# Attention in a graph network kernel: seven products of quarters for values, queries and keys, and 1/z by way of memory

## The chip, the cores and the metric

The kernel runs on one core of one Trainium2 chip. The metric is the time of one execution on the device in microseconds (us); less is better. A profile is one further execution, in which the hardware records when each instruction began and ended. In the profile's words PE is TensorE (PEld its weight loads), DVE is VectorE, ACT is ScalarE, POOL is GpSimd and SP is SyncE, which here only issues DMAs.

## The reference

Everything is float32. `x` has 1250 rows (nodes, later tokens) of 768 numbers. Two graph attention layers come first, then a transformer block with attention and a mixture of eight experts. Cut to what is touched here:

```python
x = x + gat_layers(layernorm(x), edges)            # 41250 edges
y = layernorm(x)
y = y + attention(layernorm(y, g1, b1))
y = y + moe(layernorm(y, g2, b2))                  # 8 experts, the top 2 of each token
out = x + y

def attention(a):                                  # T = 1250, H = 12 heads of HD = 64
    q, k, v = split((a @ Wqkv).reshape(T, 3, H, HD))
    scores = einsum('qhd,khd->hqk', q, k) * HD ** -0.5
    return einsum('hqk,khd->qhd', softmax(scores), v).reshape(T, D) @ Wproj
```

## The kernel before

**Sizes.** D = 768 columns are DC = 6 pieces of P = 128; the 1250 rows are NT = 10 tiles of T = 125. DH = 384. The matrix engine contracts over the partitions, so the normed rows are kept turned over: `yT` is 128 x 6 x 1250, the transposed input of the attention; the graph stage makes it tile by tile (L597 to L600). `v`, the values, is 125 x 10 x 768, rows on partitions. `wv` (the values' weights) and `wp` (Wproj) share one slot of the pool `wpool`, so `wp` is loaded after the last use of `wv`. `aT` is the attention's output, transposed like `yT`.

**Values (L653 to L660).** `value_rows(t)` makes one tile of 125 rows: two halves of 384 columns, six accumulated products each, evicted from PSUM by ACT.

**Queries and keys (L626 to L645).** `queries_keys(p)` serves a pair of heads p (0 to 5). It loads 128 columns of the keys' weights and 128 of the queries' (`wqk`), then goes through the 1250 rows in three chunks of 417, 417 and 416 columns (`CHUNKS`). For each chunk it makes keys and then queries with six accumulated products each. The keys use the PSUM bank with the tag "mb", the queries the one with the tag "pz", and ACT evicts each with a multiply, which puts the factor 1/8 (HD to the power -0.5) on the queries. It is a Python generator that yields after each product, so the caller (`go`, L647) hands out one product at a time among other work.

**A unit (L665 to L738)** is a pair of heads p and a chunk k of 417 queries; there are 18, in the order p, k. Its methods:
- `scores(j)`: for tile j of 125 keys, one product per head into a double bank `st`; ACT copies it to `sT` in a ring of 15 slots; DVE keeps the running maximum `most` (L687), which reads `st` itself.
- `top()`: eight transposes of `most` on PE and a reduction on DVE give one maximum per query; `row()`: eight more products spread it over the partitions into the bank `mb`.
- `weights(j)`: DVE subtracts `mb` (L708), ACT takes the exponential (L709), POOL adds up the ten tiles into `acc` (L714).
- `values(j)`: products of the weights with `v` into the bank `pav`. `sums` multiplies `acc` by ones, which gives z, the sum of a query's weights, on every partition of the head (bank `pz`). `divide()`: DVE takes 1/z of 128 x 417 (L737) and multiplies (L738).

**Order.** PE's instructions in the attention are in the order of the program text (`manual_schedule`, L744 and L764). The instructions of the other engines are put in order by a scheduler, except where `keep_in_program_order` pins one. First come two tiles of values, then all of the first pair's queries and keys, then the ten scores of unit 0, each followed by a tile of values (L745 to L753). Then the loop over units (L756): the head of a unit is two products of the next pair's queries and keys, `top` of the unit, `divide` of the one before, four more products, the first score of the next unit, and `row`. After the head it goes by two tiles at a time: the next unit's two scores, two products of queries and keys in the first three rounds, the weights two tiles ahead, the values. So the 36 products of a pair are spread over the three units before it is used, twelve in each. The last pair's three units have none to do.

**Queues.** SP issues the loads of `wqk` and, later, half of the reload of the rows `xs` from memory (L915); ACT issues the other half between its own instructions. POOL's queue carries the zero fill of `xd` (L618 to L624): eight large DMAs from one tile of zeros, and a small one; they prepare the experts' slots, which are filled and read after the attention. After the attention the projection takes `aT` by tiles (`product`, L925), adds it to the rows and goes on to routing and experts.

Of the kernel before, what the change touches and what calls it, by code (L numbers as in the profile page):

```python
# [27 lines left out]
def gnn_ffn_kernel(  # L28
# [69 lines left out]
    xsd = dram.tile([N, D], F32, name="xsd")  # L98
    xd = dram.tile([NE * REG + P, RW], F32, name="xd")
# [503 lines left out]
    attn = late.enter_context(tc.tile_pool(name="attn", bufs=1))  # L603
    aT = attn.tile([P, DC, N], F32, name="aT")
    with tc.tile_pool(name="att", bufs=2) as ap, \
            tc.tile_pool(name="aps", bufs=2, space=PSUM) as aps, \
            tc.tile_pool(name="apm", bufs=1, space=PSUM) as apm, \
            tc.tile_pool(name="apa", bufs=1, space=PSUM) as apa:
# [7 lines left out]


        zero = ap.tile([P, RW], F32, name="zero", bufs=1)  # L618
        nc.gpsimd.memset(zero, 0.0)  # L619
        nc.gpsimd.memset(zero[:, D:D + 1], float(NOWHERE))  # L620
        for e in range(NE):
            nc.gpsimd.dma_start(xd[e * REG:(e + 1) * REG, :].rearrange("(p r) d -> p r d", p=P),
                                zero[:, None, :].to_broadcast([P, REG // P, RW]))
        nc.gpsimd.dma_start(xd[NOWHERE:NOWHERE + P, :], zero)  # L624

        def queries_keys(p):  # L626

            wqk = ap.tile([P, DC, 2, P], F32, tag="wqk", name="wqk", bufs=1)
            for i in (1, 0):
                nc.sync.dma_start(wqk[:, :, i, :], Wqkv[:, i * D + p * P:i * D + (p + 1) * P].rearrange(  # L630
                    "(c p) f -> p c f", p=P))
            qk = ap.tile([P, 2, N], F32, tag="qk", name="qk")
            yield qk
            for c0, w in CHUNKS:
                for i in (1, 0):
                    if i == 1:
                        pq = apm.tile([P, 2, 512], F32, tag="mb", name="pk")[:, 0, :]
                    else:
                        pq = apa.tile([P, 512], F32, tag="pz", name="pq")
                    for c in range(DC):  # L640
                        nc.tensor.matmul(pq[:, :w], wqk[:, c, i, :], yT[:, c, c0:c0 + w],  # L641
                                         start=(c == 0), stop=(c == DC - 1))
                        if c == DC - 1:
                            nc.scalar.mul(qk[:, i, c0:c0 + w], pq[:, :w], 1.0 if i == 1 else HD ** -0.5)
                        yield None  # L645
# [98 lines left out]
        with tc.manual_schedule(engines={mybir.EngineType.PE}):  # L744
            for t in range(BEFORE):  # L745
                value_rows(t)
            for _ in steps:
                pass
# [417 lines left out]
```

## Time and profile before

| | us |
|---|---|
| median of three runs (lowest to highest) | 1517.28 (1515.45 to 1519.91) |
| profiled execution, its own time | 1518.66 |
| profiled execution, span of the core | 1516.8 |
| busy in the span: PE | 1437.4 (95%) |
| busy in the span: PE weight loads, beside it | 784.6 |
| busy in the span: DVE | 808.4 (53%) |
| busy in the span: ACT | 574.4 (38%) |
| busy in the span: POOL | 418.4 (28%) |
| mean clock granted to PE, of full | 0.965 |

The span divides into the graph layers (to 554), the front of the attention with values, first queries and keys and first scores (554 to 673), the units (673 to 1180.7), and projection, routing and experts (to the end). By these stages:

| us from the start | PE busy | DVE busy | ACT busy | POOL busy | PE clock | GB/s |
|---|---|---|---|---|---|---|
| 554 to 673 | 116.80 | 15.83 | 22.44 | 9.05 | 1.00 | 293 |
| 673 to 1080 | 401.53 | 315.57 | 241.04 | 247.39 | 1.00 | 12 |
| 1080 to 1180.7 | 90.61 | 80.64 | 60.74 | 63.88 | 0.95 | 39 |

The parts of a profile are read as follows. The rows by engine divide the span into 40 slices and give the busy share of each in tenths; the row PEclk gives the clock of PE in tenths of full. A group's line has the line of the code, engine and operation, what it writes and reads with the shapes (partitions x elements), how often, the busy time in all and the mean in ns, and the idle time of the engine just ahead of these instructions. A line of the timeline has the start, the duration, the engine and the operation; x8 says that eight like instructions are drawn together, and a bracket names what a wait ended with. A line of windows has the stretch, its length, and the busy time and count of PE, PEld, DVE, ACT and POOL; after them the clock of PE, the share of the DMA engines that were busy and GB/s.

### The profile page before, as it was taken

The numbers are of one execution on the slowest core, as the hardware profiler recorded it, in microseconds if no ns is written. First come the engines' busy times: TensorE is split into PE (matmuls) and PEld (weight loads), VectorE is DVE, ScalarE is ACT, GpSimd is POOL, SyncE is SP. The second block draws the span as 40 slices with busy tenths as digits, with TensorE's granted clock in tenths as the row PEclk, the third lists the DMA queues.
The fourth block names the chain that finished last, engine by engine and source line by source line (L and its number), as shares of the span: only waits on it lengthen the run. The fifth ranks groups of instructions, "written<-read, shape, count | busy, mean of one in ns | idle before, by whom it ended". The sixth has DMA issues, their size and how long they took to land. (4 is left out here: it accounts for less than half of the span.)

```text
span 1516.8 us, 15936 instructions
## 1 busy us (share of the span) xinstructions
PE 1437.4 (95%) x5990; PEld 784.6 (52%) x5990; DVE 808.4 (53%) x1287; ACT 574.4 (38%) x915; POOL 418.4 (28%) x278
## 2 busy tenths in 40 slices
PE   6787999999999999999999999999988999899997
PEld 4574555556555555553343344344333666665654
DVE  6688456434036650127778778777878654111111
ACT  4220613205116521226646656655656223221211
POOL 5000000000000010006656655665666222222222
PEclk9758999999999999999999999999999998899999
DMA  7000020000021129940000000000030323565653
GB/s 208 22 2 11 11 73 0 0 28 5 3 100 42 60 81 383 373 152 0 22 1 0 22 1 21 1 22 0 4 99 1 134 107 136 215 234 171 229 187 124
DMA packets 48198, 124.58 MB, mean 82 GB/s; under 512 B 5629, under 2 KB 22207, under 8 KB 48120
## 3 DMA queue, kind: packets, MB, share of 16 engines
q1 hardware_dynamic: 31468, 57.35, 11.6%
q0 software_dynamic: 11968, 56.21, 10.2%
q10 hardware_dynamic: 4684, 9.99, 2.2%
q8 instruction: 48, 0.79, 0.2%
q14 instruction: 30, 0.25, 0.0%
HBM read 70.46 MB, written 57.55 MB: 84 GB/s over the span
## 5 line engine op out<-in xcount | busy, mean ns | idle before, releaser
L714 POOL TENSOR_TENSOR acc<-acc,sT 125x834 f32<-125x834 f32 (+1 forms) x139 | 272.9, 1963 | 10.9
L526 PE MATMUL pagg<-h,wt 125*125 125x385 f32 (+1 forms) x800 | 263.5, 486 | 0.4 <-DVE wt L519 0.4
L687 DVE TENSOR_TENSOR most<-most,st 125x834 f32<-125x834 f32 (+1 forms) x144 | 146.9, 1020 | 107.1 <-ACT sT L681 104.2
L526 PEld LDWEIGHTS pagg<-h,wt 125*125 125x125 f32 x800 | 147.0, 187 | 104.7 <-DVE wt L519 3.5
L708 DVE TENSOR_TENSOR sT<-sT,mb 125x834 f32<-125x834 f32 (+1 forms) x180 | 174.1, 1014 | 22.6 <-PE mb L703 22.6
L709 ACT ACTIVATE sT<-sT 125x834 f32<-125x834 f32 (+1 forms) x180 | 158.4, 900 | 49.3 <-DVE sT L708 48.9
L681 ACT COPY sT<-st 125x834 f32<-125x834 f32 (+1 forms) x180 | 151.6, 848 | 53.9 <-PE st L678 52.1
L678 PE MATMUL st<-qk 64*125 64x417 f32 (+1 forms) x720 | 164.8, 558 | 4.0 <-DVE most L687 4.0
L722 PE MATMUL pav<-sT,v 125*64 125x417 f32 (+1 forms) x720 | 151.8, 534 | 9.4 <-ACT sT L709 9.4
L619 POOL MEMSET zero<- 128x771 f32 x1 | 0.7, 740 | 529.7 <-PE ptr L143 529.7
L714 POOL TENSOR_TENSOR acc<-sT 125x834 f32<-125x834 f32 (+1 forms) x18 | 35.4, 1964 | 275.9 <-ACT sT L709 275.9
L678 PEld LDWEIGHTS st<-qk 64*125 64x125 f32 x720 | 56.8, 185 | 99.4 <-issue 43.2
L722 PEld LDWEIGHTS pav<-sT,v 125*64 125x64 f32 x720 | 42.8, 137 | 106.3 <-issue 44.4
L900 PE MATMUL poe<-we,hT 128*128 128x384 f32 x264 | 89.8, 486 | 0.0
L641 PE MATMUL pq<-yT,wqk 128*128 128x417 f32 (+1 forms) x216 | 88.1, 534 | 0.0
L867 PE MATMUL phe<-xT,we 128*128 128x384 f32 (+1 forms) x288 | 86.6, 460 | 0.0
L929 PE MATMUL po<-wp,aT 128*125 128x384 f32 x240 | 86.5, 497 | 0.0
L641 PE MATMUL pk<-yT,wqk 128*128 128x417 f32 (+1 forms) x216 | 84.0, 526 | 0.0
L206 PE MATMUL ph<-gw,xnT 128*125 128x384 f32 x240 | 81.6, 500 | 0.8 <-DMA gw<-in_L_gnn_W_dram 0.8
L657 PE MATMUL pv<-wv,yT 128*125 128x384 f32 x240 | 79.9, 490 | 1.4 <-issue 1.4
L206 PE MATMUL ph<-gw,x1T 128*125 128x384 f32 x240 | 79.2, 491 | 0.0
L530 DVE RECIPROCAL rz<-pagg 125x1 f32<-125x1 f32 x20 | 3.3, 166 | 141.4 <-PE pagg L526 141.4
(225 smaller groups left out, 1718.5 us busy)
## 6 DMA issues: line engine op xcount, KB each, us to landing
xd<-zero POOLq DMA_DIRECT2D x8, 3855.0 KB, 15.7
we<-in_L_ffn_W_dram SPq DMA_DIRECT2D x16, 1152.0 KB
xr<-xd SPq DMA_DIRECT2D x25, 385.5 KB
gw<-in_L_gnn_W_dram SPq DMA_DIRECT2D x2, 2304.0 KB
wqk<-in_L_ffn_Wqkv_dram SPq DMA_DIRECT2D x12, 384.0 KB
xres<-in_x_dram SPq DMA_DIRECT2D x10, 375.0 KB
xsd<-xres ACTq DMA_DIRECT2D x10, 375.0 KB
xn<-in_x_dram SPq DMA_DIRECT2D x9, 336.0 KB
```

The source lines that it names most:

```text
L206: nc.tensor.matmul(po[:, s, :DH], xT[:, c, t * T:(t + 1) * T], w[:, c, s * DH:(s + 1) * DH], start=(c == 0), stop=(c == DC - 1))
L526: nc.tensor.matmul(po[:, s, :DH + s], ws[j][:, (d - d0) * T:(d - d0 + 1) * T], h[:, j, s * DH:(s + 1) * DH + s], start=(j == 0), stop=(j = ...
L641: nc.tensor.matmul(pq[:, :w], wqk[:, c, i, :], yT[:, c, c0:c0 + w], start=(c == 0), stop=(c == DC - 1))
L678: nc.tensor.matmul(st[:T, i, :w], self.qk[r, 1, j * T:(j + 1) * T], self.qk[r, 0, self.c0:self.c0 + w], start=True, stop=True)
L681: nc.scalar.copy(s[:, :, :w], st[:T, :, :w])
L687: nc.vector.tensor_tensor(self.most[:, :, :w], prev[:, :, :w], st[:T, :, :w], ALU.max)
L708: nc.vector.tensor_tensor(s[:, :, :w], s[:, :, :w], self.mb[:T, :, :w], ALU.subtract)
L709: nc.scalar.activation(s[:, :, :w], s[:, :, :w], AF.Exp)
L714: nc.gpsimd.tensor_tensor(self.acc[:, :, :w], prev[:, :, :w], s[:, :, :w], ALU.add)
L722: nc.tensor.matmul(self.pav[r, :w], v[:, j, hd0:hd0 + HD], s[:, i, :w], start=(j == 0), stop=(j == NT - 1))
L867: nc.tensor.matmul(ph[:, :n * P], w1[:, c, f * P:(f + 1) * P], xT[:, c, :], start=(c == 0), stop=(c == DC - 1))
L900: nc.tensor.matmul(po[:, d, :DH], hT[:, f, s * P:(s + 1) * P], w2[:, f, d * DH:(d + 1) * DH], start=(f == 0), stop=(f == FC - 1))
```

## The change

**Seven products in place of eight.** A product of two matrices cut into quarters needs eight products of quarters. The new code makes seven, of sums and differences of quarters, and puts the result together by additions (`seven`). The contraction of 768 is cut into two halves of KH = 3 pieces, the 1250 rows into two halves of NH = 625, and the weights' columns into two halves: 384 each for the values, and queries and keys (128 each) for a pair of heads. One of the seven products is three accumulated matrix instructions. Values: five rounds (a tile of the first half of the rows with the matching one of the second) of 21 products of 384 columns, which stand in place of 24. Queries and keys: two pieces of 313 and 312 columns, each with 21 products. A round has one ACT copy (product 1, kept in `u1`) and seven DVE additions, each of which reads PSUM and an earlier part and writes a part or the result.

**The sums** are POOL's. `left_sums` makes three new matrices and changes one quarter of the weights in place; they lie in the memory of `aT`, under the name `spare`. `right_sums` does the same with `yT` and makes `t2`, `t3` and `t4`. The left sums of the values and all right sums come first on POOL, then two memsets, the first pair's left sums, and the zero fill's DMAs. `t2` and `t3` are in a pool that closes after the values; two POOL copies put them into `kept`, in the slot of `wv` and `wp`. The pool `sx` then takes their memory for five of the fifteen score slots, which are now tags of their own. `wp` is loaded before unit 15.

**Order.** `go(steps, 1)` hands out one product of seven (three matrix instructions): two in the head of a unit and one in each of the first three rounds. A pair has 14 products for 15 such places. FREE and BOUND give the order of the seven and the PSUM bank of each: m and n are the two halves of "mb", z is "pz" and v is "pav". In the front all values' first round precedes the first pair's queries and keys, and the other four rounds follow the ten scores, as even as may be.

**1/z.** `divide` now has ACT copy z and the unscaled output out of PSUM (to `zs` and `aT`). SP writes one row of z per head to memory (`zd`), and reads them back as 120 partitions of 7 (`self.z`). One unit later, in the round j = 4, `invert` takes the reciprocal on DVE, writes it to memory (`zr`) and reads it back twice, once for each head's 64 partitions (into `kept`, or into `yT` for the last three units). `scale`, after the next unit's `top`, multiplies on POOL. The last unit keeps the reciprocal and the multiply of before. The factor 1/8 is now in the exponential.

The pools `att` and `attn` now take over memory tile by tile (`reuse_waits="tile"`), and `most` and `acc` have one buffer where they had two. The functions and blocks taken out are printed above; what is put in, and the lines of the units:

```diff
...
+    ZW = 420
+    zd = dram.tile([3 * H // 2, 2, ZW], F32, name="zd")
+    zr = dram.tile([3 * H // 2, 2, ZW], F32, name="zr")
...
+        spare = aT.rearrange("p c n -> p (c n)")
+        KH = DC // 2
+        NH = N // 2
+        def parts(flat, w, n):
+            return [flat[:, i * KH * w:(i + 1) * KH * w].rearrange("p (c k) -> p c k", c=KH) for i in range(n)]
+        def left_sums(a, w, flat, pin=False):
+            place = tc.keep_in_program_order if pin else lambda ins: ins
+            s1, s2, s4 = parts(flat, w, 3)
+            a11, a12, a21, a22 = (a[:, c:c + KH, f:f + w] for f in (0, w) for c in (0, KH))
+            place(nc.gpsimd.tensor_tensor(s1, a21, a22, ALU.add))
+            place(nc.gpsimd.tensor_tensor(s2, s1, a11, ALU.subtract))
+            place(nc.gpsimd.tensor_tensor(s4, a12, s2, ALU.subtract))
+            place(nc.gpsimd.tensor_tensor(a21, a11, a21, ALU.subtract))
+            return [a11, a12, s4, a22, s1, s2, a21]
+        y11, y12, y21, y22 = (yT[:, c:c + KH, n0:n0 + NH] for c in (0, KH) for n0 in (0, NH))
+        t4 = ap.tile([P, KH, NH], F32, name="t4", bufs=1)
+        def right(t2, t3):
+            return [y11, y21, y22, t4, y12, t2, t3]
+        def right_sums(t, t2, t3):
+            q = slice(t * T, (t + 1) * T)
+            nc.gpsimd.tensor_tensor(t3[:, :, q], y22[:, :, q], y12[:, :, q], ALU.subtract)
+            nc.gpsimd.tensor_tensor(y12[:, :, q], y12[:, :, q], y11[:, :, q], ALU.subtract)
+            nc.gpsimd.tensor_tensor(t2[:, :, q], y22[:, :, q], y12[:, :, q], ALU.subtract)
+            nc.gpsimd.tensor_tensor(t4[:, :, q], y21[:, :, q], t2[:, :, q], ALU.subtract)
+        FREE = ["1m", "6n", "2z", "7v", "5m", "4n", "3z"]
+        BOUND = ["1m", "2n", "6z", "7z", "4z", "5m", "3n", "1z", "2z", "6z", "7m", "4n", "5z", "3z"]
+        def seven(order, operands, np_, w, o11, o12, o21, o22):
+            def part(i):
+                return ap.tile([P, DH], F32, tag=f"u{i}", name=f"u{i}", bufs=1)[:np_, :w]
+            u4 = None
+            p1, u2, u3 = (part(i) for i in (1, 2, 3))
+            for i, name in order:
+                if name == "m":
+                    two = apm.tile([P, 2, 512], F32, tag="mb", name="mq")
+                if name in "mn":
+                    b = two[:np_, "mn".index(name), :w]
+                else:
+                    b = apa.tile([P, 512], F32, tag={"z": "pz", "v": "pav"}[name], name="q")[:np_, :w]
+                for c in range(KH):
+                    lhs, rhs = operands(int(i) - 1, c)
+                    nc.tensor.matmul(b, lhs, rhs, start=(c == 0), stop=(c == KH - 1))
+                if i == "5":
+                    u4 = part(1)
+                if i == "1":
+                    nc.scalar.copy(p1, b)
+                for o, u in {"2": [(o11, p1)], "6": [(u2, p1)], "7": [(u3, u2)], "4": [(o21, u3)],
+                             "5": [(u4, u2), (o22, u3)], "3": [(o12, u4)]}.get(i, []):
+                    nc.vector.tensor_tensor(o, b, u, ALU.add)
+                yield None
+        QW = -(-NH // 2)
+        PIECES = [(0, QW), (QW, NH - QW)]
+        def queries_keys(p, ys, free):
+            wqk = ap.tile([P, DC, 2 * P], F32, tag="wqk", name="wqk", bufs=1)
+            for i in (0, 1):
+                nc.sync.dma_start(wqk[:, :, i * P:(i + 1) * P], Wqkv[:, (1 - i) * D + p * P:(1 - i) * D + (p + 1) * P].rearrange(
...
+            ws = left_sums(wqk, P, spare[:, (4 + p % 2) * N:], pin=True)
...
+            for i, (c0, w) in enumerate(PIECES):
+                h0, h1 = slice(c0, c0 + w), slice(NH + c0, NH + c0 + w)
+                yield from seven(FREE if free else BOUND[7 * i:7 * i + 7],
+                                 lambda k, c: (ws[k][:, c, :], ys[k][:, c, h0]), P, w,
+                                 qk[:, 1, h0], qk[:, 1, h1], qk[:, 0, h0], qk[:, 0, h1])
         def go(steps, n):
...
+        def value_rows(t, ws, ys):
+            return seven(FREE, lambda k, c: (ys[k][:, c, t * T:(t + 1) * T], ws[k][:, c, :]), T, DH,
+                         v[:, t, :DH], v[:, t + NU, :DH], v[:, t, DH:], v[:, t + NU, DH:])
...
+        zs = ap.tile([P, ZW], F32, name="zs", bufs=1)
+        nc.vector.memset(zs, 1.0)
+        ZQ = 7
+        ZP = 2 * ZW // ZQ
+        def inverses(n):
+            at = n % 2 * ZW
+            if n < len(units) - NCK:
+                return kept[:, 2 * KH * NH + at:2 * KH * NH + at + ZW]
+            return yT.rearrange("p c n -> p (c n)")[:, at:at + ZW]
+        RING = 15
+        rings = [ap] * NT + [None] * (RING - NT)
...
+                self.first = (p * NCK + k) * NT
...
-                s = ap.tile([T, 2, CW], F32, tag="sT", name="sT", bufs=15)
+                r = (self.first + j) % RING
+                s = rings[r].tile([T, 2, CW], F32, tag=f"sT{r}", name="sT", bufs=1)
...
-                    self.most = ap.tile([T, 2, CW], F32, tag="most", name="most")
+                    self.most = ap.tile([T, 2, CW], F32, tag="most", name="most", bufs=1)
...
             def weights(self, j):
...
-                nc.scalar.activation(s[:, :, :w], s[:, :, :w], AF.Exp)
+                nc.scalar.activation(s[:, :, :w], s[:, :, :w], AF.Exp, scale=HD ** -0.5)
...
-                    self.acc = ap.tile([T, 2, CW], F32, tag="acc", name="acc")
+                    self.acc = ap.tile([T, 2, CW], F32, tag="acc", name="acc", bufs=1)
...
-            def divide(self):
+            def divide(self, n):
...
+                self.o = aT[:, self.p, self.c0:self.c0 + w]
+                if n + 1 == len(units):
+                    nc.vector.reciprocal(zs[:, :w], self.pz[:, :w])
+                    nc.vector.tensor_tensor(self.o, self.pav[:, :w], zs[:, :w], ALU.mult)
+                    return
+                nc.scalar.copy(zs[:, :w], self.pz[:, :w])
+                nc.scalar.copy(self.o, self.pav[:, :w])
+                for i in range(2):
+                    nc.sync.dma_start(zd[n, i:i + 1, :], zs[i * HD:i * HD + 1, :])
+                self.z = small.tile([ZP, ZQ], F32, tag="z", name="z", bufs=1)
+                nc.sync.dma_start(self.z, zd[n].rearrange("i (a b) -> (i a) b", b=ZQ))
+            def invert(self, n):
+                tc.keep_in_program_order(nc.vector.reciprocal(self.z, self.z))
+                nc.sync.dma_start(zr[n].rearrange("i (a b) -> (i a) b", b=ZQ), self.z)
+                self.rz = inverses(n)
+                for i in range(2):
+                    nc.sync.dma_start(self.rz[i * HD:(i + 1) * HD, :], zr[n, i:i + 1, :].to_broadcast([HD, ZW]))
+            def scale(self):
+                tc.keep_in_program_order(nc.gpsimd.tensor_tensor(self.o, self.o, self.rz[:, :self.w], ALU.mult))
+        with tc.tile_pool(name="tsum", bufs=1, reuse_waits="tile") as tp:
+            t2, t3 = (tp.tile([P, KH, NH], F32, name=f"t{i}") for i in (2, 3))
+            ws = left_sums(wv, DH, spare)
+            for t in range(NU):
+                right_sums(t, t2, t3)
+            zero = spare[:, 3 * N:3 * N + RW]
+            tc.keep_in_program_order(nc.gpsimd.memset(zero, 0.0))
+            tc.keep_in_program_order(nc.gpsimd.memset(zero[:, D:D + 1], float(NOWHERE)))
+            steps = queries_keys(0, right(t2, t3), True)
+            qks = [next(steps)]
+            for e in range(NE):
+                tc.keep_in_program_order(nc.gpsimd.dma_start(
+                    xd[e * REG:(e + 1) * REG, :].rearrange("(p r) d -> p r d", p=P),
+                    zero[:, None, :].to_broadcast([P, REG // P, RW])))
+            tc.keep_in_program_order(nc.gpsimd.dma_start(xd[NOWHERE:NOWHERE + P, :], zero))
+            with tc.manual_schedule(engines={mybir.EngineType.PE}):
+                for _ in value_rows(0, ws, right(t2, t3)):
+                    pass
+                for _ in steps:
+                    pass
+                rest = [r for t in range(1, NU) for r in [value_rows(t, ws, right(t2, t3))] * len(FREE)]
+                u = Unit(0, 0, qks[0])
+                for j in range(NT):
+                    u.scores(j)
+                    for r in rest[len(rest) * j // NT:len(rest) * (j + 1) // NT]:
+                        next(r)
+            kept = wpool.tile([P, DC, D], F32, tag="w", name="kept").rearrange("p c d -> p (c d)")
+            ys = right(*parts(kept, NH, 2))
+            nc.gpsimd.tensor_copy(ys[5], t2)
+            nc.gpsimd.tensor_copy(ys[6], t3)
+        sx = ring.enter_context(tc.tile_pool(name="sx", bufs=1, reuse_waits="tile"))
+        rings[NT:] = [sx] * (RING - NT)
...
+        waiting = []
...
-                    steps = queries_keys(p + 1)
+                    steps = queries_keys(p + 1, ys, False)
...
+                else:
+                    wp = load_big_weight(Wproj, "wp")
...
             with tc.manual_schedule(engines={mybir.EngineType.PE}):
-                go(steps, 2)
+                go(steps, 1)
...
-                    last.divide()
-                go(steps, DC - 2)
+                    last.divide(n - 1)
+                for old in waiting:
+                    old.scale()
+                go(steps, 1)
                 if nxt is not None:
...
                     if j < 6:
-                        go(steps, 2)
+                        go(steps, 1)
...
+                    if j == 4 and last is not None:
+                        last.invert(n - 1)
+                        waiting = [last]
...
-        last.divide()
+        last.divide(n)
+        for old in waiting:
+            old.scale()
...
```

## The prediction

> **What bounds the kernel now.** I began with the page's rows by time: TensorE (PE) is over 90% busy from slice 7 to slice 28, which holds the whole attention, and its clock there is full.
>
> ```profile
> PE   6787999999999999999999999999988999899997
> PEclk9758999999999999999999999999999998899999
> ```
>
> Next the groups, for who else is near the bound, and what each removed instruction takes.
>
> ```profile
> L714 POOL TENSOR_TENSOR acc<-acc,sT 125x834 f32<-125x834 f32 (+1 forms) x139 | 272.9, 1963 | 10.9
> L708 DVE TENSOR_TENSOR sT<-sT,mb 125x834 f32<-125x834 f32 (+1 forms) x180 | 174.1, 1014 | 22.6 <-PE mb L703 22.6
> L641 PE MATMUL pq<-yT,wqk 128*128 128x417 f32 (+1 forms) x216 | 88.1, 534 | 0.0
> L737 DVE RECIPROCAL rz<-pz 128x417 f32<-128x417 f32 (+1 forms) x17 | 46.8, 2755 | 0.0
> L738 DVE TENSOR_TENSOR aT<-pav,rz 128x417 f32<-128x417 f32 (+1 forms) x17 | 10.0, 590 | 0.5
> ```
>
> Every fp32 product is two instructions (216 where the code has 108), and a mean of 534 ns is a latency: consecutive ones start 350 ns apart (weight loads at 573.18, 573.53, ...), 0.84 ns a column. Third, the order in time of one unit of attention. Fifteen of the eighteen units with query/key work start 28.9 us apart; here is the second half of one.
>
> ```profile
> 776.20 1.67 PE L678 MATMUL st<-qk 64*125 64x417 f32 x8
> 776.39 2.89 DVE L708 TENSOR_TENSOR sT<-sT,mb 125x834 f32<-125x834 f32 x3
> 777.80 1.67 PE L641 MATMUL pq<-yT,wqk 128*128 128x417 f32 x4
> 779.19 1.02 DVE L687 TENSOR_TENSOR most<-most,st 125x834 f32<-125x834 f32 x1
> 780.66 1.02 DVE L687 TENSOR_TENSOR most<-most,st 125x834 f32<-125x834 f32 x1 [0.45 <-ACT sT L681]
> 780.95 1.76 PE L678 MATMUL st<-qk 64*125 64x417 f32 x8
> 791.24 2.76 DVE L737 RECIPROCAL rz<-pz 128x417 f32<-128x417 f32 x1
> ```
>
> PE has no gap, but VectorE (DVE) has none either from the first subtraction (767.05) to 780.2: a pair of scores needs its bank freed by the maximum two before it, and the one that frees the second bank at 781.68 is on time by 0.1 us. The 2.76 us reciprocal is in the unit's head, where DVE waits anyway. Last, the clock: the last three units have no query/key work, and PE idles in them.
>
> ```profile
> 1110.00:1113.00 3.00, 1.26 (x8) 0.49 (x6) 3.00 (x4) 1.92 (x3) 0.00 (x0) 1.00 0.99 255
> 1113.00:1116.00 3.00, 2.27 (x8) 0.49 (x8) 3.00 (x4) 1.51 (x3) 1.22 (x1) 0.67 0.19 60
> 1116.00:1120.00 4.00, 4.00 (x12) 1.46 (x12) 3.34 (x4) 3.27 (x5) 3.84 (x3) 0.50 0.00 0
> ```
>
> After 3 us with PE 1.26 us busy the clock (third column from the right) is halved for some 7 us.
>
> **Part 1, the front (554.5 to the first maxima transposes at 672.97).** Values: 240 instructions of 384 columns become 210. They start 0.330 us apart (24 from 643.13 to 651.06): 69.3 us. First pair's queries and keys: 72 x 0.350 = 25.2 becomes 84 of 312.5 columns x 0.84 ns = 0.262: 22.0. The ten score pairs stay at 0.97 each, 9.7, and one first step of the next pair is 6 x 0.262 = 1.6. But today PE starts values at 555.8, ahead of the last transposes (562.1); in the changed order the first product follows them, and waits until ScalarE (ACT) has evicted the last of yT, at 564.9. So 564.9 + 69.3 + 22.0 + 9.7 + 1.6 = 667.5, against 672.97: -5.5. PE will have idled from 554.5 to 564.9 but for 0.83 us. Here a rule bears: the Trainium skill, "TensorE: Matmul & The Clock Gate" (Part 1, the HAM clock gate), says that one idle window of about 3.4 us halves the clock and one busy window restores it. The rule would charge 1.7 us (half speed for one window), the row 3.5 (for 7 us); I take 2.5: **-3.0**.
>
> The sums go on GpSimd (POOL), idle there. A sum of two operands takes 1.96 us for 834 elements, 2.35 ns each. The values' left sums (4 x 1152 elements, 10.8 us) can start once the last weights are made on DVE (521.8), ending at 532.6; of 20 right sums (0.88 each), the last four wait for the last eviction and end at 568.4; memsets and the first left sums of the pair (0.84 + 4 x 0.90) at 572.9. The pair's products begin at about 581: 8 us of cover; gone, each us late is a us on PE. The zero-fill (8 large DMAs and a small one, 31 MB) moves past all these on POOL's queue, from 564.3 to 572.9, and ends at about 671 instead of 662; its rows are read after 1200. Into it falls the second pair's weight load (786 KB, 4 us of transfer at 750.6 when alone), wanted at 668 and issued at about 603: nothing.
>
> **Part 2, the first unit.** Two POOL copies of 1875 elements (t2, t3 to `kept`) start when the last fourth product ends, 3.6 us before the first maxima transposes; five score slots lie in the memory that they leave. No copy by POOL is in the trace. The memset (0.74 us for 771) gives 1.8 us each, the two-operand sum 4.4. "GPSIMD Engine Reference" (4.1, engine selection) puts one-input work near line rate, so I take 1.8. They end at +0.0 (+5.2 by the sum), and the first ACT copy to such a slot is at +4.3: 0 to 1; **+0.5**.
>
> **Part 3, fifteen units.** A pair of heads has three units (k = 0, 1, 2), and fourteen products of 1.57 us replace 36 matmuls: 25.2 - 22.0 = 3.2 us less PE. It is not spread evenly.
> - Head (maxima transposes to row): eight instructions and their waits took 2.99 us (790.87 to 793.86); one product takes 1.6: -1.39. The step ahead of the transposes grows from 1.40 to 1.57: +0.16.
> - Loop: three slots of 1.40 become products of 1.57, in k = 2 only two.
> - DVE loses the reciprocal and the multiply (3.35, in the head, hidden) and gets fourteen additions of PSUM and SBUF per pair. None is in the trace. The nearest row is the 417-column multiply, 0.59; with 1.02 for 834 that is 0.16 fixed + 1.03 ns a column, so 0.48 for 313, and 0.42 in a queue where 834-wide ones start 0.94 apart instead of 1.02. Bounds: nothing, where DVE has idle time, and 0.84.
> - Walking one unit with these: k = 0 and 1: PE's slots give +0.5 of which 0.3 vanishes in waits that are there now (pav waits for the exponential): -1.39 + 0.16 + 0.22 = -1.0. k = 2: three additions and the small reciprocal (0.15) come before the maximum that frees the second bank: it ends at 782.6 instead of 781.68, while PE, with no third product, arrives 1.5 us sooner: it waits 1.35 and then 1.2 us. Its first score also waits for the addition that completes the query rows, +0.65. Sum -0.24.
> - A pair: -2.24; five pairs: **-11.2** (PE alone: -16).
> - The clock in k = 2: PE is busy 0.7 of 3.25 us. By the skill's rule there is no idle window (the gap is broken by a score pair), so nothing is lost; by the row (1.26 of 3 sufficed) half speed follows, up to 3 us. The row decides on this chip; some waits hide it: 1 us each, **+5** (0 to 15).
> - The eviction now waits: ACT copies pz and pav (0.52 each) in place of its two qk evictions: even. 1/z goes through memory: two writes, a read, a DVE reciprocal of 120x7, a write, two broadcasts, 6 DMAs on SP per unit. With 3.05 us a hop (the row of `out_dram<-soon`), z lands at 2.5 + 6.2 = 8.7 us after the transposes and is inverted after the eighth subtraction, at 16.6; behind it wait two subtractions and all later maxima, and PE behind them. Cover 7.9 us. In k = 2 the read stands behind the weight load (4 us): still covered. The scaling on POOL comes a unit later, 5 us after its broadcast landed.
> - POOL: left sums 3.6 per pair and scaling 1.0 per unit before the first `acc`, which waits for ACT 10.6 us today; even.
> - The scale 1/8 moves into the exponential: nothing.
>
> **Part 4, the units without such work.** In the last three the reciprocal is not hidden: PE's row ends at 1110.36 and the subtraction starts at 1111.39, the multiply sits between the first two. Without: 1.0 + 0.4 in each of two units, and about half of the 2.2 and 0.8 us lost to the halved clock: **-4**. The third is filled with Wproj matmuls: nothing. Wproj's load moves from before the second pair to after unit 14's scaling: unit 15's small DMAs queue behind 2.4 MB (some 7 us), z lands at about 14: still before 16.6.
>
> **Part 5, the tail.** The last two 1/z lie in yT's memory, so the reload of xs (20 DMAs on SP and ACT, today from 1097.6) waits for the last scaling, 19 us into the last unit. The first rows land at +22, wanted at +25 (1184.3), and behind the waiting issues ACT has only the square root of 1189; **+0.5** (0 to 2). `first_w` then shares the rings; it is wanted 60 us later.
>
> **Sum**: -3.0 + 0.5 - 11.2 + 5 - 4 + 0.5 = -12.2. The profiled execution's span goes from 1516.8 to 1504.6, its own time from 1518.66 to 1506.5; the median shown is 1.4 lower, 1517.28, so 1505.
>
> **Rivals.**
> A, DVE's additions fit into its waits: the whole PE saving arrives, no clock loss: -5.5 - 16 - 5 = -26.5, 1491. For it: DVE is 22.7 of 28.3 us busy in a unit. Against: its idle time lies in the last two iterations.
> B, the gain is eaten by the clock: 3 us in each k = 2, 1.7 more in the front, less in part 4: -11.2 + 15 - 1.3 - 2.5 = 0, 1517. For it: the three window rows above.
> C, DVE becomes the bound in every unit: an addition takes 0.84, not 0.42. Per unit 4.67 x 0.42 = 2.0 more, 15 units, 29: less some 3 absorbed, +14, 1531. It decides from 0.66 us an addition. Against: both rows of like shape.
> That the reciprocals' wait turns into one for z would need hops of 6.9 us; I give it no chance of its own.
>
> **How the numbers follow.** Forecast 0.52 (own range 1497 to 1512), A 0.17, B 0.18, C 0.13. The range of 8 in 10 leaves out C and the lower end of A: 1489 to 1520. 0.3% (4.6 us) is about what a measurement of this kernel tells from no change: faster 0.69, same 0.18, slower 0.13.
>
> **What would show it.** First value product at 565 and half clock after it; units of 27.9, 27.9 and 28.7 us (A: 27.8 on average with full clock; C: above 29.5); PE's waits for `most` in k = 2 alone; additions of 0.48 us; no DVE idle before L821. Wrong if the additions take over 0.6, if k = 2 shows no wait, or if z arrives late.

## The result, and the profile after

The changed kernel takes 1523.85 us (median of 12 runs, 1515.75 to 1525.34) against 1516.37 us for the kernel before (12 runs). The ratio is 1.0034 (95% interval 1.0018 to 1.0050): slower by 0.3%. (The ratio is not the quotient of the two medians.) I had forecast 1505 us, with 1489 to 1520 as range, and gave "slower" 0.13.

Three marks divide a trace of either kernel: the start of the last tile's transposes (the last six products `ptr<-ident,y`), the first transposes of maxima (`ptop`), and the last ones. "Front" is from the first mark to the second, "units" from the second to the third, "tail" the rest.

| us | before | after | difference |
|---|---|---|---|
| division of the sums of tile 6 (nothing changed so far) | 512.63 | 515.07 | +2.44 |
| from there to the last transposes | 49.50 | 52.44 | +2.94 |
| front | 110.84 | 121.40 | +10.56 |
| units | 486.43 | 474.37 | -12.06 |
| tail | 357.40 | 358.89 | +1.49 |
| span | 1516.8 | 1522.2 | +5.4 |

The first row is not the change's: in the twelve traces of this study that mark lies between 511.2 and 516.7, ahead of the first changed instruction. A difference of spans between two traces can be off by several us for this alone; the stages behind that mark agree far better (the units of six kernels lie between 473.5 and 473.6).

The units gained what they were meant to gain. The front, which I had at -3.0 us, lost 13.5 with the stretch ahead of it. The page's rows by time of the changed kernel show it, slices of 38 us:

```profile
PE   5787999999999968999999999999989999899997
PEclk9757999999999988999999999999999998899999
```

Where PE was over 90% busy at full clock before, slices 15 and 16 now have a hole, with the clock down beside it. These are PE's instructions in the first part of that hole:

```profile
567.51 1.49 PE L146 MATMUL ptr<-ident,y 125*128 125x125 f32 x6 [8.42 <-DVE y L139]
570.65 4.20 PE L678 MATMUL mq<-wv,yT 128*125 128x384 f32 x6 [1.66 <-ACT yT L152]
```

and the windows of the same stretch (length; busy and count of PE, PEld, DVE, ACT, POOL; clock):

```profile
564.00:568.00 4.00, 0.49 (x3) 0.52 (x4) 3.29 (x9) 0.30 (x1) 0.00 (x0) 0.50 0.23 77
568.00:572.00 4.00, 2.35 (x7) 1.42 (x6) 0.00 (x0) 2.19 (x6) 1.25 (x2) 0.50 0.00 0
576.00:580.00 4.00, 4.00 (x7) 2.02 (x7) 0.16 (x1) 0.00 (x0) 3.84 (x5) 0.50 0.00 0
580.00:584.00 4.00, 4.00 (x14) 2.30 (x13) 1.12 (x3) 0.00 (x0) 4.00 (x6) 1.00 0.78 287
```

PE idles until the last tile is normed, waits again until ACT has evicted it, and then works at half clock until 580: 7 instructions in 4 us, then 14 at full clock. Further on, at full clock, product 5 of a round is followed by product 4 (timeline of the front):

```profile
644.96 2.20 PE L678 MATMUL mq<-aT,yT 128*125 128x384 f32 x6
648.27 2.20 PE L678 MATMUL mq<-wv,t 128*125 128x384 f32 x6 [1.11 <-DVE v L685]
```

The second starts 3.31 us after the first; where nothing is waited for, the next one starts after 1.94 to 2.04.

In the units, the groups by shape (689 to 1110 us) that answer to those shown of before:

```profile
L779 DVE TENSOR_TENSOR sT<-sT,mb 125x834 f32<-125x834 f32 x100 | 97.5, 1013 | 14.9 <-PE mb L774 14.9
L685 DVE TENSOR_TENSOR qk<-mq,u 128x313 f32<-128x313 f32 x15 | 7.2, 480 | 13.6 <-PE mq L678 13.6
L821 DVE RECIPROCAL z<-z 120x7 f32<-120x7 f32 x14 | 2.7, 193 | 0.0
```

An addition takes 0.48 us, as worked out, and the small reciprocal never waits (0.0 idle ahead of it). The fourth, fifth and sixth unit take 28.25, 28.23 and 28.45 us where they took 28.94, 28.92 and 28.91.

### The profile page after: what moved, and what is told of

It reads as the page before. It is cut to its first block, busy times and chain, and to the rows that moved or that the text cites. A ratio compares the mean times of both kernels' runs of the same rounds, so it can differ in the third digit from the quotient of the medians.

```text
span 1522.2 us, 16426 instructions
## 1 busy us (share of the span) xinstructions
PE 1414.6 (93%) x6032; PEld 794.4 (52%) x6032; DVE 813.9 (53%) x1390; ACT 572.7 (38%) x920; POOL 490.4 (32%) x345
## 5 line engine op out<-in xcount | busy, mean ns | idle before, releaser
L988 ACT ACTIVATE hT<-phe 128x384 f32<-128x384 f32 (+2 forms) x30 | 13.1, 438 | 158.0 <-PE phe L986 158.0
L986 PEld LDWEIGHTS phe<-xT,we 128*128 128x128 f32 x288 | 52.1, 190 | 33.7
L1023 DVE SCALAR_TENSOR_TENSOR sofar<-poe,weight,sofar 128x768 f32<-128x768 f32 x23 | 23.4, 1018 | 82.5 <-PE poe L1019 79.3
```

Source lines behind the costliest of these rows:

```text
L986: nc.tensor.matmul(ph[:, :n * P], w1[:, c, f * P:(f + 1) * P], xT[:, c, :], start=(c == 0), stop=(c == DC - 1))
```

## The experiments

Two theories for the front: PE waits for banks of PSUM, through the place of the pools and through two halves that are one tile; or the new work on POOL and DVE makes the front late, whatever the banks. Ten kernels, all with the full computation. Their stages:

| | median us | ratio to before (95%) | span | front | units | tail |
|---|---|---|---|---|---|---|
| changed kernel | 1523.85 | 1.0034 (1.0018 to 1.0050) | 1522.2 | 121.4 | 474.4 | 358.9 |
| e1_banks | 1525.41 | 1.0059 (1.0040 to 1.0079) | 1523.0 | 117.4 | 473.6 | 367.0 |
| e2_rotate | 1507.11 | 0.9943 (0.9910 to 0.9977) | 1506.4 | 108.3 | 473.6 | 356.5 |
| e3_both | 1511.70 | 0.9968 (0.9953 to 0.9983) | 1511.1 | 102.4 | 473.6 | 366.6 |
| e4_plain_front | 1530.17 | 1.0087 (1.0054 to 1.0121) | 1528.4 | 123.6 | 476.4 | 354.5 |
| e5_all | 1504.48 | 0.9910 (0.9881 to 0.9938) | 1500.9 | 103.7 | 473.6 | 356.8 |
| e6_plain_late_zero | 1506.53 | 0.9918 (0.9897 to 0.9939) | 1508.0 | 110.8 | 476.5 | 357.7 |
| e7_divide | 1530.33 | 1.0070 (1.0044 to 1.0096) | 1528.4 | 109.5 | 495.1 | 356.4 |
| e8_halves | 1508.39 | 0.9945 (0.9931 to 0.9959) | 1505.4 | 108.5 | 473.5 | 359.8 |
| e9_z_only | 1516.75 | 0.9993 (0.9977 to 1.0009) | 1515.9 | 110.8 | 483.0 | 357.1 |
| e10_split | 1500.34 | 0.9895 (0.9860 to 0.9931) | 1500.3 | 102.4 | 473.6 | 356.3 |

### The waits between products: e2_rotate and e8_halves

```diff
-        FREE = ["1m", "6n", "2z", "7v", "5m", "4n", "3z"]
+        def free(r):
+            return [i + "mzv"[(7 * r + at) % 3] for at, i in enumerate("1627543")]
...
```

> Only the banks of the front's products change: seven products in a row take mb (one half of it), pz and pav in turn, instead of both halves of mb after each other. Theory: PE's gaps between 1m and 6n and between 5m and 4n (10.3 us in all over the seven rounds of the front) are waits for the readers of the other half of the same double bank; with the turn they go, and the front is 10 us shorter: first maxima transposes at 679, span 1512, ratio 0.996. Rival (PE waits for ScalarE's and VectorE's evictions as such): the waits move to other products, less than 3 us gained, span 1519 or more. The start of the first product stays at 570.6 by both.

The first maxima transposes came at 676.4 (679 expected), the front at 108.3: 13.1 us shorter, more than the 10.3 that I had read off the gaps. Products 5 and 4 of a round in e2_rotate (timeline):

```profile
635.39 2.20 PE L680 MATMUL q<-aT,yT 128*125 128x384 f32 x6
637.43 2.10 PE L680 MATMUL mq<-wv,t 128*125 128x384 f32 x6
```

They start 2.04 us apart. The rest of the gain is clock: after the first product the half clock lasted 9.35 us more in the changed kernel (a stretch of 17.07 in all) and 3.74 here (10.24 in all), which at half speed is 2.8 us of work. Part of that is chance: e7_divide below has the same front, there the half clock lasted 6.11 us more after the first product, and its front is 109.5. Does PE wait because the two banks are one tile, or because an eviction needs its time? The second run keeps the order and makes two tiles of the two halves:

```diff
+        with tc.tile_pool(name="tsum", bufs=1, reuse_waits="tile") as tp, \
+                tc.tile_pool(name="apf", bufs=1, space=PSUM) as apf:
...
+                if name in "mn" and order is FREE:
+                    b = apf.tile([P, 512], F32, tag=name, name="fq")[:np_, :w]
...
```

> The order of the front's products and their banks stay those of the changed kernel, but in the front the two halves of mb are two tiles of one bank each, taken from a pool that closes before the units. It tells whether the wait is for the tile or for the time between two products. Theory: 6n waited for the copy of 1m, and 4n for the additions of 5m, because both halves are one tile, though they are two banks; with two tiles these waits go and the front is 9 to 10 us shorter than the changed kernel's 121.4: 112, units 473.6 to 475, span 1512, ratio 0.996. If it is the distance between products that matters (an eviction must be done before the next product starts): front 119 or more.

Products 5 and 4 in e8_halves:

```profile
632.03 2.20 PE L679 MATMUL fq<-aT,yT 128*125 128x384 f32 x6
634.07 2.10 PE L679 MATMUL fq<-wv,t 128*125 128x384 f32 x6
```

Front 108.5, as with the turn. So it was the tile: in the changed kernel product 6 goes to a bank that nobody reads, and yet waits for the copy of product 1, and product 4 for the additions of product 5, since both are halves of the one tile `mq`. With two tiles the same order runs through.

### The place of the pools: e1_banks, e3_both, e5_all

```diff
-            tc.tile_pool(name="aps", bufs=2, space=PSUM) as aps, \
             tc.tile_pool(name="apm", bufs=1, space=PSUM) as apm, \
             tc.tile_pool(name="apa", bufs=1, space=PSUM) as apa, \
+            tc.tile_pool(name="aps", bufs=2, space=PSUM) as aps, \
```

> Only the order in which the attention's PSUM pools are opened changes: mb, pz and pav take the banks that the graph layers' sums (pagg) leave, and no longer those of the transposes (ptr). Theory: the first value product waited for the last eviction of the transposes because its bank was theirs. It now starts at about 561 and the second follows the last transposes at about 568.4 where it started at 575.55: the first maxima transposes come 7 us earlier (682), the span is about 1515, the ratio to before about 0.999. Rival (the sums on POOL and the additions slow VectorE, and this is what makes the front late): the last transposes and all that follows them stay within 1 us of where they were, span 1521 or more.

The first maxima transposes came at 682.4, as expected, but partly by luck: 2.5 of the 6.5 us lie ahead of the first changed instruction (the division of tile 6 came at 512.55 in place of 515.07). The span did not come. The first product of the values now starts ahead of the last transposes:

```profile
557.92 2.17 PE L678 MATMUL mq<-wv,yT 128*125 128x384 f32 x6 [1.36 <-issue]
564.99 1.49 PE L146 MATMUL ptr<-ident,y 125*128 125x125 f32 x6 [4.89 <-DVE y L139]
```

In the changed kernel it stood behind them and waited for their eviction, because its bank had been theirs. The front is 4.0 us shorter. But the tail is 8.1 us longer, and there is no gain. I had followed the banks of the front only.

> Both edits together, pool order and banks in turn. Three products stand ahead of the last transposes on PE. Theory: 7 us of the start, 4 us of products in PE's former gap, 2 us of half clock and 10 us of bank waits: first maxima transposes at about 666, span about 1500, ratio 0.989. If POOL's sums and the additions on VectorE are the cause of the late front: span 1512 or more.

The first maxima transposes came at 670.9 (666 expected). The front is 102.4, and none is shorter, but the tail is 366.6: a span of 1511.1, not 1500. Who takes the banks next is the projection. Its first products (`po`) fill PE's gaps in the last unit. In e3_both (the tile's own view: duration, then first and last start):

```profile
L1050 PE MATMUL po<-wp,aT x240: 484/486/568, 1168.2 to 1265.5; 128*125 128x384 f32 x120
```

That is 23.7 us after the last maxima transposes (1144.5), when the last unit is done with `pav` and `pz`. The edit of e5_all is one more change of order:

```diff
-            tc.tile_pool(name="ppo", bufs=2, space=PSUM) as ppo, \
             tc.tile_pool(name="ppt", bufs=2, space=PSUM) as ppt, \
-            tc.tile_pool(name="ppl", bufs=2, space=PSUM) as ppl:
+            tc.tile_pool(name="ppl", bufs=2, space=PSUM) as ppl, \
+            tc.tile_pool(name="ppo", bufs=2, space=PSUM) as ppo:
```

> Pool order and banks in turn as in the run before, and the projection's PSUM pools in another order too, so that its product (po) takes the banks of the scores again and not those of mb, pz and pav. Theory: the pool order alone gave back in the tail what it won in the front, because the first projection products of the last unit then waited for the bank of that unit's pav and pz; from the last maxima transposes to the end it took 367 us where it is 357 to 359 else. It comes back to 357 to 359, front 102.4, units 473.6: span 1502 to 1504, ratio 0.990 to 0.992. If the tail is long for another reason: it stays at 366 or more, span 1511.

```profile
L1050 PE MATMUL po<-wp,aT x240: 484/486/587, 1147.8 to 1257.4; 128*125 128x384 f32 x120
```

The first `po` now starts 3.7 us after the last maxima transposes (1144.1), the tail is 356.8, and the kernel is faster than the one before and the changed one.

### The plain front: e4_plain_front and e6_plain_late_zero

Is the front worth seven products at all? The edit puts the functions of before back for the values and the first pair; `t2`, `t3` and `t4` are made by POOL without touching `y12`, which is changed once the values are done. Its core:

```diff
-                for _ in value_rows(0, ws, right(t2, t3)):
-                    pass
+                for t in range(BEFORE):
+                    value_rows(t)
...
+            pin(nc.gpsimd.tensor_tensor(t2[:, :, q], t3[:, :, q], y11[:, :, q], ALU.add))
...
+                    if p == 0:
+                        tc.keep_in_program_order(nc.gpsimd.tensor_tensor(y12, y12, y11, ALU.subtract))
```

> Values and the first pair's queries and keys are made by plain products as before, in the order of before; only pairs 1 to 5 use seven products, and 1/z goes through memory. POOL's right sums leave y12 as it is until the values are done, and come after the zero fill. Theory: the front lasts 110.8 us from the last transposes to the first maxima transposes, as before, VectorE's work on the last tiles is not slowed (0.96 us for each addition to xres), the units keep their 474.4 us: span 1516.8 - 12.1 + 1.5 = 1506, ratio 0.993. If the units' gain rests on what the front does (score slots in other memory, a later zero fill), the units come out above 478 us and the span at 1510 or more.

It missed: front 123.6, ratio 1.0087. The zero fill no longer had anything to wait for, and started 39 us earlier than in the kernel before (POOL's timeline, then VectorE's):

```profile
524.92 7.66 POOL L853 DMA_DIRECT2D xd<-aT  x8 [0.30 <-POOL aT L851]
567.67 0.96 DVE L594 TENSOR_TENSOR xres<-xres,o 125x768 f32<-125x768 f32 x1 [10.10 <-DMA xres<-in_x_dram]
```

Its 31 MB kept the last load of `x` away for 10.1 us, though that load is on another queue. The second kernel issues the zero fill after the last tile's sums:

```diff
+            right_sums(NU - 1, t2, t3)
             zero = spare[:, 3 * N:3 * N + RW]
...
-            for t in range(NU):
+            for t in range(NU - 1):
                 right_sums(t, t2, t3)
```

> The plain front again, with the zero fill issued after the sums of the last tile, where it was before, and not ahead of the last tile. Theory: the early zero fill had made the last load of x land 10.1 us late, and the first weights of queries 7.1 us late, and these alone lengthened the front; now the last transposes come 7.4 us after the last sum is divided, the front lasts 111 us, the span is 1506 to 1508, ratio 0.993. If the plain front cannot be had beside the sums for later pairs (POOL's right sums slow VectorE): front above 113, span above 1510.

As expected: last transposes 7.4 us after the last division, front 110.8, ratio 0.9918. This version has nothing of the seven products in the front and already keeps the gain of the units (two late units are 1.6 and 1.2 us longer than elsewhere; the trace has 3.41 us of half clock in each, which e5_all has not). The seven-product front at its best (e3, e5, e10) is 7 to 8 us shorter, of which its sums take 2 to 3 back ahead of the last transposes. In the whole time the intervals of e5_all, e6 and e10 overlap, so that the front is worth its seven products is shown by its stages and not by the total.

### POOL against DVE: e10_split

From the division of tile 6 to the last transposes it takes 49.5 us in before and in the two kernels that do no left or right sums early (e6, e9), and 52.4 in those with whole sums ahead of the last tile (e4, with its late load, takes 60.0). The instructions that pay are few: five of VectorE's, beside POOL's sums. The dearest, before (the first line) and in the changed kernel (timelines of the two engines):

```profile
522.49 0.68 DVE L136 TENSOR_SCALAR y<-y,mv,rstd 125x768 f32<-125x768 f32 x1
524.50 2.62 POOL L638 TENSOR_TENSOR aT<-wv 128x1152 f32<-128x1152 f32 x1 [488.71 <-DVE wt L522]
524.94 2.60 DVE L139 TENSOR_SCALAR y<-y,mv,rstd 125x768 f32<-125x768 f32 x1
```

The scaling takes 0.68 us when POOL is still, and this one delays the next tile by 1.46 of the 2.94 us. The rest is three additions to `xres` (1.17, 1.06 and 1.72 us in place of 0.96) and another scaling (1.08 in place of 0.67). The Trainium skill, "SBUF — State Buffer" (SBUF: two separate sides), says that GpSimd and such VectorE instructions as run in a two-port mode or read two operands from SBUF share one pair of ports as a lock, held for a whole instruction. A slow sharing of bandwidth could look alike here; shorter sums tell the two apart.

```diff
-            place(nc.gpsimd.tensor_tensor(s1, a21, a22, ALU.add))
...
+            cuts = [slice(0, KH)] if pin else [slice(c, c + 1) for c in range(KH)]
+            for o, l, r, op in [(s1, a21, a22, ALU.add), (s2, s1, a11, ALU.subtract),
+                                (s4, a12, s2, ALU.subtract), (a21, a11, a21, ALU.subtract)]:
+                for c in cuts:
+                    place(nc.gpsimd.tensor_tensor(o[:, c, :], l[:, c, :], r[:, c, :], op))
```

> The kernel with pool order, banks in turn and the projection's banks, and in it each of the four left sums of the values (1152 elements, 2.62 us) cut into three of 384 elements (about 0.9 us). In the traces with whole sums VectorE's scaling of tile 7 (y<-y,mv,rstd, 0.68 us) took 2.60 us, as long as the first sum. If VectorE waits for a whole instruction of POOL, that scaling now takes at most 1.6 us, the 19.5 us between the sums' division of tiles 6 and 7 become 18.5 or less (18.05 without sums), the last transposes come 1 us earlier, span 1500. If the two engines share bandwidth instead, the scaling still takes more than 2 us and the step stays 19.5.

```profile
526.13 3.22 POOL L642 TENSOR_TENSOR aT<-wv 128x384 f32<-128x384 f32 x3 [489.36 <-DVE wt L522]
526.57 0.98 DVE L139 TENSOR_SCALAR y<-y,mv,rstd 125x768 f32<-125x768 f32 x1
```

The same scaling takes 0.98 us, and the step to the next tile 18.06, as without sums. POOL's total is not less: its three pieces take 3.22 us in place of 2.62. So VectorE waits for a whole instruction of POOL, as the page has it. The last transposes gained 1.1 us against e5_all; at 0.9895 this is the lowest ratio, though not clearly below that of e5_all.

### 1/z by way of memory: e7_divide and e9_z_only

```diff
-                if n + 1 == len(units):
+                if True:
                     nc.vector.reciprocal(zs[:, :w], self.pz[:, :w])
...
-                for old in waiting:
-                    old.scale()
...
```

> Banks in turn in the front, and the division as before: the reciprocal of 128 x 417 on VectorE and the multiply, in place of 1/z by way of memory. It tells what that part of the change is worth in units whose head is shorter by 1.4 us. Theory: the reciprocal (2.76 us) now stands in front of the addition that completes the product of the head, and the maximum row waits for it: about 1.3 us more in each of fifteen units, 1.0 to 1.4 in the last ones, units 494 us in place of 473.6, span about 1526, ratio 1.007. Rival (it is hidden in the head, as I had it for the kernel before): units within 3 us of 473.6, span 1506 to 1509.

The other way round, everything else as before (each `go` as before too):

```diff
-                ws = left_sums(wqk, P, spare[:, (4 + p % 2) * N:], pin=True)
...
-                go(steps, 1)
+                go(steps, 2)
                 u.top()
...
```

> All products plain, in the order of the kernel before; of the change only 1/z by way of memory is kept (with the scaling on POOL, the scale 1/8 in the exponential, the later load of Wproj, and the sums of the last tile on POOL, which nothing reads and which only hold the zero fill in its place). By the prediction the reciprocal and its multiply are hidden in the head of the fifteen units that have query and key products: units 0 to 14 stay within 0.1 us of 28.9 each, the two after them lose 2.7 and 1.1 us as in the changed kernel: units 482 to 483, front 111, span 1513, ratio 0.998. Rival: most of the 12 us that the units gained is due to 1/z, since undoing it cost 21.6: units 0 to 14 become 28.4 or less, span 1508 or less.

In e9_z_only the units with query and key products take 28.9 us, as before: alone, the part is worth nothing there. The two units after them are 1.4 and 2.1 us shorter (2.7 and 1.1 expected), and the ratio is 0.9993. In e7_divide, with seven products, its absence costs 21.6 us against e2_rotate. The head of a unit there (timelines of the two engines):

```profile
823.99 2.76 DVE L812 RECIPROCAL zs<-pz 128x417 f32<-128x417 f32 x1
826.66 0.42 DVE L687 TENSOR_TENSOR qk<-mq,u 128x312 f32<-128x312 f32 x1
827.13 0.97 PE L750 MATMUL st<-qk 64*125 64x417 f32 x4 [1.68 <-DVE qk L687]
```

The addition stands behind the reciprocal, and PE behind the addition. That unit then ran into half clock for 3.41 us and took 30.76 in place of 28.45 (29.49 in the first pair, where the clock stayed full). The units of e7_divide have seven such stretches and those of e2_rotate none, so part of the 21.6 us is clock that the waits cost. So the reciprocal was hidden in the old head, as I had it, and is not in the new one. The parts of the change don't add up singly: seven products with the old division would have lengthened the units by 8.7 us against before, both together shorten them by 12.

## Why the prediction was wrong, point by point

- **Part 1, the sum of the front's products on PE.** This step failed, by a missing term. "69.3 us", "22.0" and the rest lay the products end to end. That sum was good: from the last transposes it gives 107.9 us with the 2.5 for the clock, and the two kernels without bank waits show 108.3 and 108.5. (That it is so close is partly luck: in e2_rotate the value products start 1.94 us apart and the scores take 0.90, where I had 1.98 and 0.97; but value products next to a score start 2.03 to 2.04 apart; and the half clock costs 1.9 us there, not 2.5.) What was left out are the waits between products: 13.1 us, by e2_rotate, some 10 of them the waits themselves and the rest the longer half clock. I followed banks in the units and took them for granted in the front, where FREE puts two products in a row on the two halves of one tile.
- **Part 1, "the sums go on GpSimd (POOL), idle there".** I charged them only where PE might wait for them. They cost 2.94 us, through DVE. DVE's norms of the last tiles are on the path that ends in the last transposes, and a 0.68 us instruction took 2.60. The trace of before does not show the two engines at work together in that stretch; the page cited above would have told me to ask.
- **Part 1, the late start.** Its effect was right (the first product follows the last eviction, half clock after it). Its cause is not the new order, to which I put it down, but the pools' place; e1_banks shows it, and that it could be undone.
- **The signs.** First value product at 565: it came at 570.65, which is 3.1 us after the last transposes where I had 2.8. Units of 27.9, 27.9 and 28.7: 28.25, 28.23, 28.45. Additions of 0.48, waits for `most` in k = 2 alone, no idle time ahead of the small reciprocal: as said.
- **Part 2**, +0.5: the copies take 1.74 us each (1.8 expected), and the first unit takes 28.27 us, no more than the others with k = 0 (28.25): nothing was lost.
- **Part 3**, -11.2 and +5 for the clock. The fifteen units gained 9.0 us, 1.84 in a full pair where I had 2.24 less the clock. In the head one product takes 1.78 us, not 1.6, so that gives -1.2 and not -1.39. The clock loss did not come, and so all the units together gained 12.1 us where Parts 2 to 4 had 9.7: two misses that cancel in part, the second the larger. Here is k = 2 in the changed kernel, timeline and window:

```profile
850.18 0.97 PE L748 MATMUL st<-qk 64*125 64x417 f32 x4 [0.96 <-DVE most L758]
```

```profile
848.00:851.00 3.00, 2.04 (x12) 0.58 (x8) 3.00 (x6) 3.00 (x5) 2.84 (x3) 1.00 0.03 4
```

  The waits for `most` are there, and only in k = 2, but they are 0.96 and 0.14 us (0.90 in the last such unit) where I had 1.35 and 1.2, PE stays busy for 2.04 of 3 us, and the clock at 1.00. I had let the row of 1.26 busy us in 3 decide against the page on the clock gate; the busy share in k = 2 was not like that row's.
- **1/z.** The time line held: inverted 16.4 to 17.8 us after the maxima transposes in these units (16.6 expected), no idle time of DVE ahead of it. What I never priced is its absence; e7_divide did.
- **Part 4**, -4: -3.1 here, -3.9 in e2, e3, e5, e8 and e10; the 0.8 between them goes with one stretch of 3.41 us at half clock that the last but one unit has here and not in those.
- **Part 5**, +0.5: +1.5, but the eight other kernels whose projection kept its banks have tails of 354.5 to 359.8, so nothing can be read from it.
- **Rivals.** None had the mechanism. A (additions fit in the waits) and C (DVE becomes the bound) were both about the units; my rival for slower was C, with 0.84 us an addition, and they take 0.48. B named the clock in k = 2. The loss sat in the front, where I had only thought of gains, of the start and of the clock.

## What to carry to other kernels

Before summing products on PE, write down for each which tile of PSUM it goes to, who last read any part of that tile, and whose bank it was under the pool before: waits of up to 1.2 us in each round ate all that the smaller count of products brought in the front, and another choice of tiles gave it back. Work put on an idle GpSimd was not free here, because VectorE was on the path; if it must lie there, cut it into short instructions. Undo each part of a change by itself in both surroundings: taking the reciprocal out was worth nothing in the fifteen old units with query and key products, and 21.6 us in the new ones.

## What the hardware showed that I had not expected

- Half clock comes in multiples of 3.41 us (3.41 to 17.07 in these attentions). The Trainium skill, "TensorE: Matmul & The Clock Gate" (Part 1), gives a free-running window of 3413 ns. In each of the twelve traces every stretch begins and ends on such a grid, but for the last one's end, which is the end of the trace. In e7_divide, k = 2 of the second to the fifth pair went to half clock at 829.2, 917.9, 1006.7 and 1095.4, 88.7 us apart, which is 26 windows; that of the first pair, with the same 1.68 us gap of PE, did not. So 1.68 us of idle PE can be enough, where the page speaks of an idle window. The place on the grid may decide (the four gaps began within 0.3 us of an edge of it, the fifth 0.8 us behind one), but five cases don't show it. The longest single gap is not the measure either: in the window ahead of the half clock at 1091.84 in e6_plain_late_zero PE was busy for 1.56 of 3.41 us, with gaps of 0.96 and 0.90, while the 0.96 us gap of k = 2 in the changed kernel never led to half clock. Which share of a window decides is open.
- In e4_plain_front one load on SP's queue kept VectorE waiting for 10.1 us beside a 31 MB fill issued by POOL; with the fill issued later (e6) it did not.
